# Loading half of each later image as 32-token squares and turning them on VectorE, with the first layer's channels in runs of four per partition

## The chip, the core and the metric

The kernel runs on one core of one Trainium2 chip. The core has five engines that each work through their own instructions in order: TensorE (PE) does the matrix products and the transposes that go through it, VectorE (DVE) and ScalarE (ACT) do elementwise work and read the products out of PSUM, GpSimd (POOL) does elementwise work and issues DMAs, and SyncE (SP) only issues DMAs. Weight loads of PE are listed as an engine of their own (PEld). The metric is the device time of one execution in microseconds.

## The reference, cut to what matters

The input x is eight images of 32 by 32 tokens with 512 channels, in float32. Two layers follow one another. The first normalises x over groups of 16 channels of an image, makes queries, keys and values from it with one 512 x 1536 weight, attends with eight heads of 64 channels, and adds the projected result to x:

```python
def _group_norm(x, scale, bias):
    xg = x.reshape(b, h * w, NUM_GROUPS, c // NUM_GROUPS)
    mu = jnp.mean(xg, axis=(1, 3), keepdims=True)
    var = jnp.var(xg, axis=(1, 3), keepdims=True)
    xn = (xg - mu) * jax.lax.rsqrt(var + EPS)
    return xn.reshape(b, h, w, c) * scale + bias
qkv = _group_norm(x, gn_scale, gn_bias).reshape(b, seq, c) @ w_qkv + b_qkv
weight = softmax(einsum('bhld,bhsd->bhls', q / 8, k / 8))
out = einsum('bhls,bhsd->bhld', weight, v)
x = x + out.transpose(0, 2, 1, 3).reshape(b, seq, c) @ w_out + b_out
```

The second layer (layer norm, a query projection with a depthwise 7 x 7 convolution that gives sampling places, attention to the sampled tokens, and a one-matrix MLP) is not touched. What the change touches is how x reaches the layout that the first layer's products need, with channels on partitions and tokens along the row.

## The kernel before, in words

**Rounds and units.** The first layer goes image by image. A round `b` is the attention of image `b`, and it has `per` = 32 units: four pairs of heads (`hp`) times eight tiles of 128 queries (`qt`). One unit pushes one tile of queries of one head pair: PE makes the scores `sc` (16 matmuls), DVE takes their maxima `nmax` (two reductions over 128 x 1024), ACT takes the exponentials `e` (two of 128 x 1024), DVE turns them in 32 x 32 blocks into `sq` (two more 128 x 1024), SP moves the blocks to their places in `et` by DMA (16 DMAs for two units), and three units later PE multiplies `et` with the values into `av`. There are two PSUM tiles for `sc`, one per head of the pair, so PE can start a unit's scores only when the exponentials of the unit before have been read. There is one PSUM tile for `av`; every fourth unit DVE scales it into `attT`, and only then can the next `av` begin. Beside this, each unit has a place for one more product of PE (`mm`): queries, keys and values of the next head pair, the output projection of the image before, or a chunk of the next layer's convolution input.

**The order is written out by hand.** `at(place, step)` files a step under a place, counted in units from the kernel's first; steps of equal place keep the order in which they were filed. In each unit `push` first gives out the scores, maxima and exponentials, then runs the steps with places up to 0.8 into the unit (`before`), then the two turns of `e` and their DMAs, then the steps from 0.8 to 1 (`after`). So a DVE step at place 10.9 stands behind the turns of unit 10 and ahead of the maxima of unit 11. `nc` is wrapped in `InOrder`, so every engine keeps the order of the program.

**How x gets its layout.** `norm_steps` (line 569) prepares image `b + 1` during round `b`. `turn(t)` takes one tile of 128 tokens x 512 channels, `x`, which `load_x` (line 519) has fetched on POOL's queue in 128 rows of 2 KB; PE transposes its four 128 x 128 parts into a PSUM tile and ACT copies that into `xT` (128 partitions x 4 chunks x 512 tokens, `blk` 0 or 1). There are NX = 2 buffers for `x` and NX_T = 3 for `xT`. Each turn then issues the load of the tile two further on; that DMA stands on POOL's queue and waits until PE has read the buffer. `two_tiles(i)` takes statistics of two turned tiles on DVE (four `bn_stats` of 256 tokens), `gather`, `means`, `deviations` and `factors` make the factors per channel, with two products by `gmat` that sum over groups, and `norm` applies them. The list `norm_places` (line 1001) says when: the eight turns at units 8.4, 8.45, 16.4, 16.45, 22.4, 22.45, 23.4 and 23.45, the statistics at 9.85, 17.86, 22.86 and 23.95, the rest from 23.97 to 26.85. Image 0 is prepared in the same way ahead of round 0.

**What else stands on the engines there.** From round 1's unit 26 on, the next layer's convolution of earlier images runs in the gaps, in chunks (`conv_chunk`, line 919, with `conv_plan`): each of its 49 taps is either a `part_x` of ACT that POOL adds into `oa`, or one `od` instruction of DVE, which reads the padded input `pad_x` and the sum. In rounds 1 to 7 the output projection of the image before runs too (`out_steps`, line 708): per tile a load of `xr` and an addition on POOL, a sum, statistics and `hat` on DVE (`summed` at 0.85 and `norm` at 0.85 of a unit), and two more products of `hat` on POOL.

**Weights.** `w3` holds the three thirds of `w_qkv` with channel `c * 128 + p` on partition `p`, chunk `c`; `gsc` and `gbi`, scale and bias of the group norm, are laid out the same way by `load_cols`.

Of the kernel before, what the change touches and what calls it, by code (L numbers as in the profile page):

```python
# [17 lines left out]
P = 128  # L18
# [230 lines left out]
def attention_then_deformable_attention(  # L249
# [118 lines left out]
    def at(place, step):  # L368
        due.append((place, len(due), step))
# [140 lines left out]
    with ExitStack() as l0:  # L510
# [6 lines left out]
        xs = {}  # L517

        def load_x(b, t):
            if b < B:  # L520
                xs[b, t] = work.tile([P, C], F32, tag="x", name="x", bufs=NX)
                nc.gpsimd.dma_start(xs[b, t], x_tok[b][ts(t, P), :])


        x2 = work.tile([P, NC, QB], F32, tag="xT", name="x2", bufs=NX_T)
# [3 lines left out]
            xs[0, NQT + t] = x2[:, t, :]  # L529
            nc.sync.dma_start(xs[0, NQT + t], x_tok[0][ts(NQT + t, P), :])  # L530
        w3 = [kept(name) for name in ("wA", "wB", "wC")]
        gsc = load_cols(wp, gn_scale, "gsc")
        gbi = load_cols(wp, gn_bias, "gbi")
        bqkv = load_cols(wp, b_qkv, "bqkv")
        for i in (1, 0, 2):
            nc.sync.dma_start(w3[i], by_chunk(w_qkv)[:, :, ts(i, C)])
        bout = load_row(wp, b_out, "bout")
        room_w = {}

# [5 lines left out]
        def load_quarter(w, c):  # L545
# [7 lines left out]

        gmat = wp.tile([P, P], F32, tag="gmat", name="gmat")
        nc.gpsimd.memset(gmat, 1.0 / GRP)
        g3 = gmat.rearrange("p (g c) -> p g c", c=GRP)
        ng = P // GRP
        nc.gpsimd.affine_select(
            out=g3, in_=g3, pattern=[[-GRP, ng], [0, GRP]], compare_op=ALU.is_ge,
            fill=0.0, base=0, channel_multiplier=1,  # L560
        )
        nc.gpsimd.affine_select(
            out=g3, in_=g3, pattern=[[GRP, ng], [0, GRP]], compare_op=ALU.is_ge,
            fill=0.0, base=GRP - 1, channel_multiplier=-1,
        )
        att = MovedAttention(nc, ident, ps_mm, ps_sc, ps_av, work, dram, 1)
        xTs, qkv, vals = {}, {}, {}
# [1 line left out]
        def norm_steps(b, start, places):  # L569

            room = {}

            def turn(t):
                blk, i = divmod(t, NQT)
                if i == 0:
                    xTs[b, blk] = work.tile([P, NC, QB], F32, tag="xT", name="xT", bufs=NX_T)
                if t == 0:
                    room["stats"] = work.tile([P, NC, NT // 2, 6], F32, tag="stats", name="stats", bufs=1)
                ps = mm_tile()
                for c in range(NC):  # L580
                    nc.tensor.transpose(ps[:, ts(c, P)], xs[b, t][:, ts(c, P)], ident)
                nc.scalar.copy(xTs[b, blk][:, :, ts(i, P)], ps.rearrange("p (c q) -> p c q", q=P))
                if b > 0:
                    load_x(b + (t + NX) // NT, (t + NX) % NT)
                elif t < NX:
                    load_x(1, t)

            def two_tiles(i):
                blk, half = divmod(i, NQT // 2)
                for c in range(NC):  # L590
                    nc.vector.bn_stats(
                        room["stats"][:, c, i, :], xTs[b, blk][:, c, ts(half, 2 * P)]
                    )


            def gather():
                mv = room["mv"] = work.tile([P, NC, 2], F32, tag="mv", name="mv")
                stats = room["stats"]
                for c in range(NC):
                    nc.vector.bn_aggr(mv[:, c, :], stats[:, c, :, :].rearrange("p s f -> p (s f)"))  # L600

            def means():
                mv = room["mv"]
                ps = mm_tile()
                for m in range(2):
                    half = ds(m * HD, HD)
                    nc.tensor.matmul(
                        ps[half, 0:NC], lhsT=gmat[:, half], rhs=mv[:, :, 0], start=True, stop=True
                    )
                mu = room["mu"] = work.tile([P, NC], F32, tag="mu", name="mu")  # L610
                nc.vector.tensor_copy(mu, ps[:, 0:NC])
                dev = room["dev"] = work.tile([P, NC], F32, tag="dev", name="dev")
                nc.vector.tensor_tensor(dev, mv[:, :, 0], mu, ALU.subtract)
                nc.vector.tensor_tensor(dev, dev, dev, ALU.mult)
                nc.vector.tensor_tensor(dev, dev, mv[:, :, 1], ALU.add)

            def deviations():
                ps = mm_tile()
                for m in range(2):
                    half = ds(m * HD, HD)  # L620
                    nc.tensor.matmul(
                        ps[half, 0:NC], lhsT=gmat[:, half], rhs=room["dev"], start=True, stop=True
                    )
                room["rs"] = work.tile([P, NC], F32, tag="rs", name="rs")
                rstd(room["rs"], ps[:, 0:NC], 1e-6)

            def factors():
                nc.vector.tensor_tensor(room["rs"], room["rs"], gsc, ALU.mult)
                room["add"] = work.tile([P, NC], F32, tag="nadd", name="nadd")
                nc.vector.tensor_tensor(room["add"], room["mu"], room["rs"], ALU.mult)  # L630
# [15 lines left out]

            steps = [
                *(lambda t=t: turn(t) for t in range(NT)),
                *(lambda i=i: two_tiles(i) for i in range(NT // 2)),
                gather, means, deviations, factors,  # L650
                *(lambda blk=blk: norm(blk) for blk in range(NQB)),
            ]
            for place, what in zip(places, steps):
                at(start + place, what)

        def qkv_steps(b, hp, places):

# [261 lines left out]
        def conv_chunk(b, cb, n):  # L919
# [78 lines left out]
        ]  # L998
        first_values = (1.3, 2.3, 3.3, 4.3)
        value_places = [(-1.7, 2.3, 3.6, 4.3), (10.3, 18.3, 19.3, 20.3)]  # L1000
        norm_places = [
            *(8.4, 8.45, 16.4, 16.45, 22.4, 22.45, 23.4, 23.45),
            *(9.85, 17.86, 22.86, 23.95),
            *(23.97, 24.03, 25.03, 25.81, 25.85, 26.85),
        ]
        out_places = [3.3, 5.3, 6.3, 7.3, 11.3, 13.3, 14.3, 15.3]
# [7 lines left out]
                        start=(c == 0), stop=(c == n - 1),  # L1014
                    )

        norm_steps(0, -100, norm_places)
# [528 lines left out]
```

## Time and profile before

| what | us |
|---|---|
| median of the runs (3 runs) | 3262.32 (3259.76 to 3265.22) |
| the profiled execution | 3264.03 |
| its span, first to last instruction | 3262.3 |
| rounds 2 to 6, from 508.56 to 1821.01 in the span | 1312.45 |
| of these, PE busy | 1311.20 |
| DVE, ACT, POOL busy in them | 1126.55, 835.34, 799.47 |
| 256 transposes of x on PE, whole kernel | 37.5 |
| 64 copies of the turned tiles on ACT | 34.4 (586 ns each) |
| 60 loads of x issued by POOL | 33.3 (557 ns each) |
| 128 statistics of `xT` on DVE | 44.4 (409 ns each) |
| 276 taps `od` on DVE | 232.7 (843 ns each) |

The rows of instruction groups give the time in which at least one of a group was running, and the mean length of one. "Idle before" in such rows is time in which that engine had nothing to do before the instruction, with what ended the wait. In a timeline, the first number is the start in us from the span's beginning, the second the length of the group of like instructions. A busy PE is not PE at its peak, since matmuls are pipelined.

### The profile page before, as it was taken

The page shows a single profiled execution, that of the slowest core. Times are in us where ns is not written, and L with a number is a line of the kernel's source. Part 1 is how long each engine was busy: PE and PEld are TensorE (multiplying, and loading weights), DVE is VectorE, ACT ScalarE, POOL GpSimd, SP SyncE. Part 2 cuts the span into 40 slices and gives each one's busy share as a digit, 9 for nine tenths or more (in the row PEclk, how much of TensorE's full clock was granted, in tenths as well). Part 3 has the DMA queues.
Part 4 walks back from the last instruction along what each step waited for, and adds up shares of the span by engine and source line. Part 5 has one row for each costly group of instructions (what it writes and reads, how often), then busy time and mean ns, then how long its engine had stood idle before and what let it go on. Part 6 is the DMA issues. An engine that isn't in the chain of part 4 may idle for free.

```text
span 3262.3 us, 59564 instructions
## 1 busy us (share of the span) xinstructions
PE 3217.9 (99%) x21588; PEld 1301.2 (40%) x21588; DVE 2522.9 (77%) x3457; ACT 1780.8 (55%) x3826; POOL 1593.5 (49%) x2026
## 2 busy tenths in 40 slices
PE   8999999999999999999999999999999999999999
PEld 4444344344344444444444434333333333333333
DVE  5776778898888888788788888557868787676765
ACT  3443356566567567557657656335555555554442
POOL 1001316755764665664674577225556565653323
PEclk9999999999999999999999999999999999999999
DMA  5666766777677766676676677678777786887873
GB/s 171 169 179 162 210 181 180 211 200 186 204 196 191 203 197 177 204 211 178 181 223 183 177 216 211 180 228 272 219 240 242 228 264 211 264 259 229 265 236 130
DMA packets 479325, 674.31 MB, mean 207 GB/s; under 512 B 76828, under 2 KB 268632, under 8 KB 478776
## 3 DMA queue, kind: packets, MB, share of 16 engines
q1 hardware_dynamic: 434528, 529.53, 56.8%
q0 software_dynamic: 41136, 136.78, 13.7%
q10 hardware_dynamic: 3368, 4.20, 0.4%
q8 instruction: 171, 2.80, 0.4%
q14 instruction: 122, 1.00, 0.1%
HBM read 263.17 MB, written 138.69 MB: 123 GB/s over the span
## 4 chain that ended last, share of the span: by engine, by line
PE 89%; DVE 3%; ACT 2%; DMA 2%; POOL 1%; issue 1%; SPq 1%; POOLq 0%; DVEq 0%; ACTq 0%
PE mm L54 55%; PE sc L54 17%; PE av L54 17%; ACT e L54 1%; DVE nmax L54 1%; SPq L54 1%; DMA et<-sq_d 1%; DVE sq L54 1%; POOL oa L54 0%; DVE chunk L54 0%; DMA w<-in_L_conv_w_out_dram 0%; DMA sq_d<-sq 0%; POOL xr L54 0%; DMA row<-mid,ii 0%; ACT part_x L54 0%
## 5 line engine op out<-in xcount | busy, mean ns | idle before, releaser
L54 ACT ACTIVATE e<-sc,nmax 128x1024 f32<-128x1024 f32 (+1 forms) x1024 | 803.0, 797 | 531.4 <-DVE nmax L54 524.7
L54 DVE TENSOR_REDUCE nmax<-sc 128x1 f32<-128x1024 f32 (+1 forms) x640 | 750.2, 1212 | 291.3 <-PE sc L54 286.0
L54 POOL TENSOR_TENSOR oa<-part_x,oa 128x256 f32<-128x256 f32 x852 | 639.4, 751 | 542.5 <-ACT part_x L54 496.4
L54 DVE STREAM_TRANSPOSE sq<-e 128x1024 f32<-128x1024 f32 x640 | 764.3, 1225 | 118.5 <-ACT e L54 97.7
L54 ACT ACTIVATE part_x<-pad_x,dww_x 128x256 f32<-128x256 f32 x852 | 441.2, 545 | 259.9 <-POOL oa L54 258.4
L54 PE MATMUL sc<-k,q 64*64 64x512 f32 x4096 | 512.3, 603 | 8.8 <-ACT e L54 6.7
L54 PE MATMUL av<-et,v 128*64 128x256 f32 x4096 | 499.2, 386 | 11.7 <-DMA et<-sq 4.5
L54 PEld LDWEIGHTS av<-et,v 128*64 128x64 f32 x4096 | 273.7, 137 | 328.8 <-issue 162.1
L54 POOL TENSOR_TENSOR mv<-mv,minus_half 128x1 f32<-128x1 f32 x128 | 76.3, 596 | 389.0 <-DVE mv L54 388.0
L54 PEld LDWEIGHTS sc<-k,q 64*64 64x64 f32 x4096 | 137.5, 132 | 314.6 <-issue 208.4
L54 POOL TENSOR_TENSOR chunk<-parts,chunk 128x256 f32<-128x256 f32 x240 | 185.3, 772 | 137.2 <-ACT parts L54 123.2
L54 DVE SCALAR_TENSOR_TENSOR od<-pad_x,dww_x,od 128x256 f32<-128x256 f32 x276 | 232.7, 843 | 5.5
L54 PE MATMUL mm<-wo,attH 128*64 128x512 f32 x1024 | 233.7, 598 | 0.0
L54 PE MATMUL mm<-wC,xT 128*64 128x256 f32 x2048 | 232.1, 379 | 0.0
L54 PE MATMUL mm<-xT,wB 128*64 128x512 f32 x1024 | 230.7, 592 | 0.6 <-DVE xT L54 0.6
L54 PE MATMUL mm<-hat_h,wA 128*64 128x512 f32 x1024 | 230.9, 593 | 0.0
L54 PE MATMUL mm<-xT,wA 128*64 128x512 f32 x1024 | 230.7, 592 | 0.0
L54 PE MATMUL mm<-w,attT 128*64 128x512 f32 x1024 | 230.1, 592 | 0.3 <-DMA w<-in_L_conv_w_out_dram 0.3
L54 PE MATMUL mm<-wm,zT 128*64 128x512 f32 x976 | 220.7, 592 | 0.5 <-ACT zT L54 0.5
L54 ACT ACTIVATION_READ_ACCUMULATOR e<-sc,nmax 128x1 f32 x1024 | 209.1, 204 | 0.0
L54 PEld LDWEIGHTS mm<-wC,xT 128*64 128x64 f32 x2048 | 148.0, 137 | 77.7 <-issue 6.4
L54 PE MATMUL mm<-w,hat_x 128*64 128x512 f32 x768 | 170.2, 593 | 0.0
(198 smaller groups left out, 3457.6 us busy)
## 6 DMA issues: line engine op xcount, KB each, us to landing
et<-sq SPq DMA_DIRECT2D x2048, 128.0 KB
sq_d<-sq SPq DMA_DIRECT2D x128, 512.0 KB
et<-sq_d SPq DMA_DIRECT2D x128, 512.0 KB
inv<-rs_d SPq DMA_DIRECT2D x250, 128.0 KB
xr<-mid POOLq DMA_DIRECT2D x64, 256.0 KB
xr<-in_x_dram POOLq DMA_DIRECT2D x62, 256.0 KB
x<-in_x_dram POOLq DMA_DIRECT2D x60, 256.0 KB
out_dram<-res POOLq DMA_DIRECT2D x60, 256.0 KB
```

The lines of the kernel that those rows point to most:

```text
L54: return self.tc.keep_in_program_order(op(*args, **kwargs))
```

## The change

Two kinds of loading take the place of one. For images 1 to 7, the first four tiles (`blk` 0) are fetched by `load_squares` in four DMAs of 64 KB each: DMA `r` brings channels `128 r` to `128 r + 127` of the tile's 128 tokens onto the 32 partitions `32 r` to `32 r + 31`, as four runs of 512 bytes a partition. One DVE transpose in 32 x 32 blocks then writes the tile's part of `xT`, reading every fourth column, with no PE transpose, no PSUM tile and no ACT copy. Partition `p` so holds channels `4 p` to `4 p + 3`, and everything of the first layer that lies along channels follows: the rows of `w_qkv`, `gsc` and `gbi` are loaded in runs of four channels a partition, the PE transposes that remain (image 0, and tiles 4 to 7 of the later images) read every fourth column of `x`, and `gmat` sums over 4 partitions instead of 16, after which a DVE reduction sums the four columns; the factors become one number per partition.

The places move too. In rounds 0 to 6 the four DVE transposes stand at units 1.9, 4.9, 10.9 and 15.9, the first statistics at 11.85 instead of 9.85, the squares of tiles 2 and 3 between 2.6 and 9.6, those of the next image's tiles 0 and 1 between 24.6 and 31.6, and the loads of tiles 4 and 5 at 11.6 and 16.6. The PE turns of tiles 4 to 7 stay at 22.4, 22.45, 23.4 and 23.45.

```diff
         def load_x(b, t):
-            if b < B:
+            xs[b, t] = work.tile([P, C], F32, tag="x", name="x", bufs=NX)
+            nc.gpsimd.dma_start(xs[b, t], x_tok[b][ts(t, P), :])
+
+        def load_squares(b, t, r):
+            if r == 0:
                 xs[b, t] = work.tile([P, C], F32, tag="x", name="x", bufs=NX)
-                nc.gpsimd.dma_start(xs[b, t], x_tok[b][ts(t, P), :])
+            nc.gpsimd.dma_start(
+                xs[b, t][ts(r, SQ)].rearrange("q (s c) -> q s c", s=NSQ),
+                x_tok[b][ts(t, P), ts(r, P)].rearrange("(s q) c -> q s c", s=NSQ),
+            )
...
-        gsc = load_cols(wp, gn_scale, "gsc")
-        gbi = load_cols(wp, gn_bias, "gbi")
+        def load_runs(v, name):
+            t = wp.tile([P, NC], F32, tag=name, name=name)
+            nc.sync.dma_start(t, v.rearrange("(p c) -> p c", c=NC))
+            return t
+
+        gsc, gbi = load_runs(gn_scale, "gsc"), load_runs(gn_bias, "gbi")
...
-            nc.sync.dma_start(w3[i], by_chunk(w_qkv)[:, :, ts(i, C)])
+            nc.sync.dma_start(w3[i], w_qkv.rearrange("(p c) o -> p c o", c=NC)[:, :, ts(i, C)])
...
-        g3 = gmat.rearrange("p (g c) -> p g c", c=GRP)
+        span = GRP // NC
+        g3 = gmat.rearrange("p (g c) -> p g c", c=span)
...
+                if b > 0 and blk == 0:
+                    nc.vector.transpose(
+                        xTs[b, blk][:, :, ts(i, P)].rearrange("p c (s q) -> p s c q", s=NSQ),
+                        xs[b, t].rearrange("p (s i c) -> p s c i", s=NSQ, c=NC),
+                    )
+                    return
                 ps = mm_tile()
                 for c in range(NC):
-                    nc.tensor.transpose(ps[:, ts(c, P)], xs[b, t][:, ts(c, P)], ident)
+                    nc.tensor.transpose(
+                        ps[:, ts(c, P)], xs[b, t].rearrange("p (i c) -> p c i", c=NC)[:, c], ident
+                    )
                 nc.scalar.copy(xTs[b, blk][:, :, ts(i, P)], ps.rearrange("p (c q) -> p c q", q=P))
-                if b > 0:
-                    load_x(b + (t + NX) // NT, (t + NX) % NT)
-                elif t < NX:
-                    load_x(1, t)
+                if b > 0 and t + NX < NT:
+                    load_x(b, t + NX)
...
-                mu = room["mu"] = work.tile([P, NC], F32, tag="mu", name="mu")
-                nc.vector.tensor_copy(mu, ps[:, 0:NC])
+                mu = room["mu"] = work.tile([P, NC], F32, tag="mu", name="mu")[:, 0:1]
+                nc.vector.tensor_reduce(mu, ps[:, 0:NC], AX.X, ALU.add)
...
-                rstd(room["rs"], ps[:, 0:NC], 1e-6)
+                room["one"] = work.tile([P, NC], F32, tag="dev", name="one")[:, 0:1]
+                nc.vector.tensor_reduce(room["one"], ps[:, 0:NC], AX.X, ALU.add)
+                rstd(room["one"], room["one"], 1e-6)
...
+            if b > 0:
+                for t in range(NX):
+                    at(start + load_places[t], lambda t=t: load_x(b, NQT + t))
+                    for r, place in enumerate(square_places[t]):
+                        at(start + place, lambda t=t, r=r: load_squares(b, NX + t, r))
+            if b + 1 < B:
+                for t in range(NX):
+                    for r, place in enumerate(square_places[NX + t]):
+                        place = places[t] + 0.001 if b == 0 else place
+                        at(start + place, lambda t=t, r=r: load_squares(b + 1, t, r))
...
-        norm_places = [
+        first_norm_places = [
             *(8.4, 8.45, 16.4, 16.45, 22.4, 22.45, 23.4, 23.45),
             *(9.85, 17.86, 22.86, 23.95),
             *(23.97, 24.03, 25.03, 25.81, 25.85, 26.85),
         ]
+        square_places = [
+            (2.6, 3.6, 5.6, 6.6),
+            (6.65, 7.6, 8.6, 9.6),
+            (24.6, 25.6, 26.6, 27.6),
+            (28.6, 29.6, 30.6, 31.6),
+        ]
+        load_places = (11.6, 16.6)
+        norm_places = [
+            *(1.9, 4.9, 10.9, 15.9, 22.4, 22.45, 23.4, 23.45),
+            *(11.85, 17.86, 22.86, 23.95),
+            *(23.97, 24.03, 25.03, 25.81, 25.85, 26.85),
+        ]
```

More of the change, by code (lines that the diff above doesn't have):

```diff
@@ L555, in attention_then_deformable_attention @@
         nc.gpsimd.memset(gmat, 1.0 / GRP)
-        g3 = gmat.rearrange("p (g c) -> p g c", c=GRP)
-        ng = P // GRP
+        span = GRP // NC
+        g3 = gmat.rearrange("p (g c) -> p g c", c=span)
+        ng = P // span
         nc.gpsimd.affine_select(
-            out=g3, in_=g3, pattern=[[-GRP, ng], [0, GRP]], compare_op=ALU.is_ge,
+            out=g3, in_=g3, pattern=[[-span, ng], [0, span]], compare_op=ALU.is_ge,
             fill=0.0, base=0, channel_multiplier=1,
@@ L562, in attention_then_deformable_attention @@
         nc.gpsimd.affine_select(
-            out=g3, in_=g3, pattern=[[GRP, ng], [0, GRP]], compare_op=ALU.is_ge,
-            fill=0.0, base=GRP - 1, channel_multiplier=-1,
+            out=g3, in_=g3, pattern=[[span, ng], [0, span]], compare_op=ALU.is_ge,
+            fill=0.0, base=span - 1, channel_multiplier=-1,
         )
@@ L609, in means @@
                     )
-                mu = room["mu"] = work.tile([P, NC], F32, tag="mu", name="mu")
-                nc.vector.tensor_copy(mu, ps[:, 0:NC])
+                mu = room["mu"] = work.tile([P, NC], F32, tag="mu", name="mu")[:, 0:1]
+                nc.vector.tensor_reduce(mu, ps[:, 0:NC], AX.X, ALU.add)
                 dev = room["dev"] = work.tile([P, NC], F32, tag="dev", name="dev")
-                nc.vector.tensor_tensor(dev, mv[:, :, 0], mu, ALU.subtract)
+                nc.vector.tensor_scalar(dev, mv[:, :, 0], mu, None, ALU.subtract)
                 nc.vector.tensor_tensor(dev, dev, dev, ALU.mult)
@@ L624, in deviations @@
                 room["rs"] = work.tile([P, NC], F32, tag="rs", name="rs")
-                rstd(room["rs"], ps[:, 0:NC], 1e-6)
+                room["one"] = work.tile([P, NC], F32, tag="dev", name="one")[:, 0:1]
+                nc.vector.tensor_reduce(room["one"], ps[:, 0:NC], AX.X, ALU.add)
+                rstd(room["one"], room["one"], 1e-6)
             def factors():
-                nc.vector.tensor_tensor(room["rs"], room["rs"], gsc, ALU.mult)
+                nc.vector.tensor_scalar(room["rs"], gsc, room["one"], None, ALU.mult)
                 room["add"] = work.tile([P, NC], F32, tag="nadd", name="nadd")
-                nc.vector.tensor_tensor(room["add"], room["mu"], room["rs"], ALU.mult)
+                nc.vector.tensor_scalar(room["add"], room["rs"], room["mu"], None, ALU.mult)
                 nc.vector.tensor_tensor(room["add"], gbi, room["add"], ALU.subtract)
@@ L1015, in warm @@
                     )
-        norm_steps(0, -100, norm_places)
+        norm_steps(0, -100, first_norm_places)
         for place in (-76.035, -74.5):
```

## The prediction

> **What bounds the kernel now.** I read the page first: how busy each engine is, and which engine the chain that ended last runs through.
>
> ```profile
> PE 3217.9 (99%) x21588; PEld 1301.2 (40%) x21588; DVE 2522.9 (77%) x3457; ACT 1780.8 (55%) x3826; POOL 1593.5 (49%) x2026
> ...
> PE 89%; DVE 3%; ACT 2%; DMA 2%; POOL 1%; issue 1%; SPq 1%; POOLq 0%; DVEq 0%; ACTq 0%
> ```
>
> PE sets the time, and its work shrinks here, so the change looks like a gain. How much is in it shows in PE's timeline of one unit with turns: here unit 16 of round 5 (the round starts at 1296.56).
>
> ```profile
> 1440.47 3.60 PE L54 MATMUL mm<-xT,wA 128*64 128x512 f32 x16
> 1444.01 1.09 PE L54 MATMUL mm<-ident,x 128*128 128x128 f32 x8
> 1445.03 1.52 PE L54 MATMUL sc<-k,q 64*64 64x512 f32 x12
> ```
>
> Two turns hold PE from 1444.01 to 1445.03, 1.02 us. Then I asked who else has no time to spare in the units to which the work goes: busy time by unit, units 11, 12, 13, 15 and 16 of round 5 (the columns: stretch, length, PE, PEld, DVE, ACT, POOL, clock, DMA).
>
> ```profile
> 1393.90:1401.09 7.19, 7.19 (x50) 2.72 (x48) 6.97 (x7) 5.20 (x10) 5.16 (x7) 1.00 0.80 237
> 1401.09:1408.28 7.19, 7.19 (x50) 2.73 (x49) 6.86 (x13) 4.27 (x9) 4.26 (x7) 1.00 0.94 284
> 1408.28:1418.90 10.62, 10.62 (x66) 3.87 (x64) 9.28 (x8) 5.32 (x12) 8.95 (x10) 1.00 0.65 183
> ...
> 1429.56:1436.74 7.18, 7.18 (x50) 2.72 (x48) 4.51 (x6) 4.26 (x9) 5.80 (x7) 1.00 0.70 208
> 1436.74:1445.03 8.29, 8.29 (x59) 3.76 (x57) 7.99 (x14) 4.79 (x10) 6.63 (x8) 1.00 0.66 172
> ```
>
> DVE has 0.2 to 0.3 us left in units 11, 12 and 16. Last, DVE's own order there, and ACT's exponentials after it.
>
> ```profile
> 1396.44 2.34 DVE L54 TENSOR_REDUCE nmax<-sc 128x1 f32<-128x1024 f32 x2
> 1398.92 2.37 DVE L54 STREAM_TRANSPOSE sq<-e 128x1024 f32<-128x1024 f32 x2
> 1401.22 0.65 DVE L54 TENSOR_TENSOR attT<-av,inv 128x512 f32<-128x512 f32 x1
> ...
> 1403.91 2.35 DVE L54 TENSOR_REDUCE nmax<-sc 128x1 f32<-128x1024 f32 x2
> ...
> 1410.10 4.19 DVE L54 SCALAR_TENSOR_TENSOR od<-pad_x,dww_x,od 128x256 f32<-128x256 f32 x3
> 1414.22 2.34 DVE L54 TENSOR_REDUCE nmax<-sc 128x1 f32<-128x1024 f32 x2
> ```
>
> ```profile
> 1406.68 1.10 ACT L54 ACTIVATE e<-sc,nmax 128x1024 f32<-128x1024 f32 x1
> ...
> 1417.70 1.10 ACT L54 ACTIVATE e<-sc,nmax 128x1024 f32<-128x1024 f32 x1
> ```
>
> From 1396.44 to 1414.22 DVE is hardly ever idle. The second exponential of unit 12 ends at 1407.78, and PE starts the next scores, which need its buffer, at 1408.28: 0.50 to spare. In unit 13 it ends at 1418.80 and the scores start at 1418.90: 0.10 to spare. PE looks full, but here DVE is as much the bound.
>
> **What is removed.** In rounds 0 to 6, two turns in unit 8 and two in unit 16: 14 pairs of 1.02 = 14.3 us of PE, if nothing else holds PE. 28 copies of 586 ns leave ACT (16.4 us), which is not the bound. The old POOL waits for PE before loads of x (173.1 us over 13 waits) end; nearly all lie in rounds 0 and 1, where POOL has no taps to do. I count 0 for them.
>
> **What is added on DVE.** Each DVE transpose of x is 128 x 512, reading every fourth float. No row has that read. The nearest two are the turn of `zT` (128 x 512, its writes 16 bytes apart) and the contiguous turn of `sq`:
>
> ```profile
> L54 DVE STREAM_TRANSPOSE zT<-l x57: 1075/1116/1156, 2261.8 to 3196.3; 128x512 f32<-128x512 f32 x57
> ...
> L54 DVE STREAM_TRANSPOSE sq<-e x640: 1195/1229/1249, 38.8 to 3204.9; 128x1024 f32<-128x1024 f32 x160
> ```
>
> Between half of 1.229 = 0.61 and 1.11 us. I take 1.11: same operation, same size, same step of 16 bytes, though on the other side.
>
> The Trainium skill (SBUF — State Buffer, the note on cachelines in "Door 1: The DMA port swizzle") says that reads within a 16-byte line run at full rate and that each step to a new line pays, and yet lists four fp32 as a step that is still free. The `zT` row paid for such a step (1.116 for half the elements of 1.229). By the list the sum below would be some 5 us lower; by the first half of the rule it stands, and PE's reads would pay too.
>
> Now by place. Unit 1.9: DVE waits 0.85 before the maxima of unit 2 (1316.37), and their exponentials leave 1.7 to spare: 0. Unit 4.9: unit 5's maxima start at 1344.28 straight behind three taps, its second exponential ends at 1348.86, the next scores start at 1350.05: 1.19 to spare against 1.11, so 0, but only just. Unit 10.9: unit 11 has 1.16 to spare against 1.11, so again 0. But the delay stays on DVE, and at 11.85 come the statistics of tiles 0 and 1, moved from 9.85 (four in 1.36 us at 1385.03). They are filed before `attT` and `summed` of the same place, so they run ahead of both; behind them wait `attT` (which the next `av` needs; 1.10 to spare), the output sum and unit 12's maxima. These come 1.11 + 1.36 = 2.47 late. What is late next: unit 12's exponentials, unit 13's taps, unit 13's maxima. PE loses 2.47 - 0.50 = 1.97 in front of unit 13 and, with 0.10 spare there, 2.37 by unit 14.
>
> Unit 15.9: again 1.11 ahead of unit 16's maxima, which already start 2.5 us after their first scores are ready. Unit 14's idle PE time cannot be won back, as POOL, ACT and DVE follow each other with 0.08 to spare in unit 15. So unit 16's exponentials come 2.47 + 1.11 = 3.58 late against 0.77 to spare (that spare lies beside the 1.02 of the turn): the next scores start 2.81 late, turn or no turn. Its 1.02 us buy nothing. Unit 18 has 0.42 to spare and can make that 3.16 if the taps of unit 17 pass the delay on whole; its exponentials lose 1.06 of ACT copies (1447.21) in front of them, so I add 0.2.
>
> Per round: -1.02 (unit 8) + 2.81 + 0.2 = +2.0 in rounds 4 to 6. Round 2 has 0.78 to spare in unit 16 and gives the same, +2.0; round 3 has 1.17, +1.6. Five rounds: +9.6. Round 1 has no convolution and only little on DVE: -2.04. In round 0 unit 8's next scores wait for `e` anyway (4.78 us against 4.58 for such a unit without a turn), so nothing comes back there; unit 12's `av` waits for `attT`, now behind the statistics, +1.4; unit 16 gives -1.02. Round 0: +0.4. Together +9.6 - 2.0 + 0.4 = +8.0.
>
> **What is added elsewhere.** POOL issues 112 squares and 32 whole loads of x instead of 60: +84 at 557 ns = 47 us, 12 a round, mostly at .6, between taps that ACT waits for. The units from 24 on have 0.5 to 1.6 to spare in round 5, and in units 9 to 11 POOL waits 1.8 to 5.4 us: 0. If POOL has no such gap, three units a round (28 to 30) could lose up to 0.5 each, 5 x 1.5 = 7.5. The squares wait for a DVE transpose 0.7 units or more before them; taps stand behind them, ACT's `part_x` behind those. They land units ahead of use (4.3 at least, 31 us): 0.
>
> PE's weight loads of the 144 transposes that stay (8 tiles of image 0, 28 of the others) now step 16 bytes. No row has this on PE. The nearest on PE are loads of `smp`, 8 bytes apart: 138 ns against 137. The other bound is the `zT` rate, half. The eight transposes of a pair take 128 ns each; twice that would add 112 x 0.128 = 14.3 us in units 22 and 23, where PE is the bound, and 32 x 0.128 = 4.1 at the start. I take the PE row, 0, and keep 18 for the range. One small reduction more on DVE (0.15) and a power of one column on POOL instead of four (0.60 for 1.04) per image, the shorter `gsc` and `gbi` loads (0.43 and 0.51 on SP at 2.65, ahead of weights that are not waited for), and `w_qkv` in the same 2 KB pieces: 0.3 less at the start, in the rounding.
>
> Sum: 3264.03 + 8 = 3272 for the profiled execution, which lies 1.7 above the median 3262.32; so 3270 for the median.
>
> **Rivals.** (1) The read of every fourth float is free on DVE: 0.61 in place of 1.11 takes 2 x 0.5 a round off five rounds, -5: 3265. For it: taps `od` read every second float and still take 442 ns at least for 256. Against: `zT`. (2) PE pays for the stepped weight loads, point of decision 137 ns becoming more than the 128 between two transposes: with half to all of 18, 3279 to 3288. (3) The other side: DVE's queue takes the additions in its gaps and PE's 14.3 come back, 3248, or half of them, 3255. For it: the places 1.9, 4.9, 10.9 and 15.9 lie in DVE's emptiest units (5.74, 4.99, 5.89 and 4.51 busy), and taps run between 442 and 2358 ns beside POOL, so a shift can shorten them: they need to lose over 2 us a round between units 10 and 17 before it is faster. Against: 0.10 and 0.08 us to spare, round after round, and round 7, which has no turns at all: its unit 16 is 7.19 long with 0.13 to spare, so even there 1.11 us more would lengthen it. That the turns of `blk` 0 leave PE is sure from the code.
>
> Why taps stretch: three took 4.19 us at 1410.10 where POOL added `xr` and `hat`, against 442 ns for the shortest. The Trainium skill (SBUF — State Buffer, "Who interferes with whom") gives the reason: DVE with two SBUF inputs and POOL share a port pair, held for a whole instruction. By it, more POOL work in these units would stretch taps further; squares are not issued in units 12 to 15, so the sum is the same.
>
> **How the numbers follow.** Forecast (DVE's delay eats the gain): 0.40, its own range 3265 to 3278. Rival 1: 0.20. Rival 2: 0.20. Rival 3: 0.20. Faster or slower means by over 0.2%, 6.5 us, about what a measurement of this kernel can tell from no change. Faster: most of rival 3, with a little of 1, 0.19. Same: 0.16 of rival 1, a fifth of the forecast (0.08): 0.24. Slower: the rest, 0.57. The range 3254 to 3285 leaves out the better half of rival 3 and the top of rival 2.
>
> **What would show it.** Right: no PE transposes of x in units 8 and 16; unit 8 at 7.2 us; the x turns on DVE near 1.11 us; unit 12 of rounds 4 to 6 near 9.2 us with PE waiting for `e` or `attT`; unit 16 not shorter than 8.3; units 22 and 23 unchanged at 8.21. Wrong: unit 16 at 7.2 and unit 12 unchanged (rival 3); turns of 0.6 us (rival 1); units 22 and 23 longer (rival 2). A change elsewhere in the span, in the second layer or before 34 us by over 3 us, is in no term of mine.

## The result, and the profile after

| | before | after |
|---|---|---|
| median of 5 runs of each, us | 3265.22 (3259.76 to 3269.47) | 3281.62 (3277.39 to 3286.43) |
| ratio of the two | | 1.0054, 95% interval 1.0038 to 1.0070 |
| a second set, 18 and 6 runs | 3263.42 (3258.66 to 3269.23) | 3277.32 (3272.45 to 3278.78) |
| ratio | | 1.0039, 95% interval 1.0026 to 1.0052 |
| profiled execution, span | 3264.03, 3262.3 | 3283.78, 3282.1 |

The changed kernel is slower by 14 to 16 us. The first two lines below are of the page of the changed kernel (busy time by engine, and the engines of the chain that ended last), the rest of its view of the tile `x` by shape (minimum, median and maximum of one instruction in ns).

```profile
PE 3224.1 (98%) x21476; PEld 1296.8 (40%) x21476; DVE 2552.9 (78%) x3493; ACT 1766.9 (54%) x3798; POOL 1634.7 (50%) x2110
...
PE 82%; POOL 5%; ACT 4%; DVE 4%; DMA 3%; issue 2%; SPq 1%; POOLq 0%; DVEq 0%; ACTq 0%
```

```profile
L54 POOL DMA_DIRECT2D x<-in_x_dram x144: 536/558/707, 1.4 to 1767.7; - x144
L54 PEld LDWEIGHTS mm<-ident,x x144: 195/212/226, 7.5 to 1775.3; 128*128 128x128 f32 x144
...
L54 DVE STREAM_TRANSPOSE xT<-x x28: 1076/1124/1139, 47.4 to 1714.8; 128x512 f32<-128x512 f32 x28
```

PE has 112 matmuls fewer and yet a busy time 6.2 us longer: time in which the matmuls of a group wait for a buffer counts as busy, as unit 13 below shows. The chain runs through PE for 82% instead of 89%; POOL, ACT and DVE have gained what it lost. A DVE turn of x takes 1.12 us, and a weight load of the transposes that are left takes 212 ns where it took 140.

Where the time went is seen unit by unit. A unit is counted from the first matmul of its scores to that of the next unit's. These are units 11 to 17 of round 5 (the round starts at 1304.63), busy time by stretch, columns as before:

```profile
1400.95:1408.14 7.19, 7.19 (x51) 2.73 (x49) 6.98 (x7) 4.41 (x9) 4.58 (x6) 1.00 0.82 233
1408.14:1416.60 8.46, 7.25 (x50) 2.72 (x48) 8.13 (x17) 4.00 (x8) 5.41 (x8) 1.00 0.93 269
1416.60:1427.90 11.30, 11.30 (x66) 4.17 (x64) 9.95 (x9) 5.97 (x12) 8.97 (x10) 1.00 0.66 177
1427.90:1438.96 11.06, 11.06 (x67) 4.05 (x65) 9.94 (x14) 6.48 (x14) 8.16 (x11) 1.00 0.68 179
1438.96:1446.14 7.18, 7.18 (x50) 2.71 (x48) 4.50 (x7) 4.25 (x9) 5.80 (x7) 1.00 0.65 198
1446.14:1453.70 7.56, 7.35 (x50) 2.96 (x48) 7.42 (x13) 3.27 (x8) 5.96 (x7) 1.00 0.61 150
1453.70:1465.45 11.75, 11.69 (x65) 4.05 (x65) 11.37 (x11) 6.95 (x13) 10.05 (x13) 1.00 0.80 264
```

Units 12, 13, 14, 16 and 17 were 7.19, 10.62, 10.65, 8.29 and 10.62 before. DVE's timeline from unit 11 into unit 13 shows why, and PE's beside it where the loss lands:

```profile
1403.48 1.12 DVE L54 STREAM_TRANSPOSE xT<-x 128x512 f32<-128x512 f32 x1
1404.53 2.31 DVE L54 TENSOR_REDUCE nmax<-sc 128x1 f32<-128x1024 f32 x2
1406.98 2.38 DVE L54 STREAM_TRANSPOSE sq<-e 128x1024 f32<-128x1024 f32 x2
1409.28 1.36 DVE L54 BATCH_NORM_STATS2 stats<-xT 128x6 f32<-128x256 f32 x4
1410.56 0.68 DVE L54 TENSOR_TENSOR attT<-av,inv 128x512 f32<-128x512 f32 x1
...
1413.28 2.35 DVE L54 TENSOR_REDUCE nmax<-sc 128x1 f32<-128x1024 f32 x2
```

```profile
1408.14 1.95 PE L54 MATMUL sc<-k,q 64*64 64x512 f32 x16
1411.29 1.95 PE L54 MATMUL av<-et,v 128*64 128x256 f32 x16 [1.21 <-DVE attT L54]
1413.07 3.60 PE L54 MATMUL mm<-xT,wB 128*64 128x512 f32 x16
1416.60 2.63 PE L54 MATMUL sc<-k,q 64*64 64x512 f32 x16
```

The turn at 1403.48 and the statistics at 1409.28 stand in one queue of DVE, with no gap behind them. `attT` begins 2.42 us into unit 12 (0.13 before), the maxima 5.14 us into it (2.82 before). PE waits 1.21 us for `attT`. Then the scores of unit 13 take 2.63 us instead of 1.95: the first half starts when the first exponential of unit 12 has freed its buffer, the second half waits for the other, so the page counts that wait as busy PE.

### The profile page after: what moved, and what is told of

It is laid out like the page before. It is cut to its first block, busy times and chain, and to the rows that moved or that the text cites. A ratio compares the mean times of both kernels' runs of the same rounds, so it can differ in the third digit from the quotient of the medians.

```text
span 3282.1 us, 59491 instructions
## 1 busy us (share of the span) xinstructions
PE 3224.1 (98%) x21476; PEld 1296.8 (40%) x21476; DVE 2552.9 (78%) x3493; ACT 1766.9 (54%) x3798; POOL 1634.7 (50%) x2110
## 4 chain that ended last, share of the span: by engine, by line
PE 82%; POOL 5%; ACT 4%; DVE 4%; DMA 3%; issue 2%; SPq 1%; POOLq 0%; DVEq 0%; ACTq 0%
PE mm L54 52%; PE sc L54 16%; PE av L54 15%; ACT e L54 3%; POOL oa L54 2%; DVE nmax L54 1%; POOL xr L54 1%; DVE sq L54 1%; POOL hat L54 1%; ACT part_x L54 1%; DMA sq_d<-sq 1%; DMA et<-sq 1%; SPq L54 1%; DMA row<-mid,ii 0%; DVE xT L54 0%
## 5 line engine op out<-in xcount | busy, mean ns | idle before, releaser
L54 PE MATMUL sc<-k,q 64*64 64x512 f32 x4096 | 528.8, 603 | 11.9 <-ACT e L54 9.3
L54 POOL DMA_DIRECT2D x<-in_x_dram x144 | 81.2, 566 | 247.1 <-DVE xT L54 139.2
```

The source lines that it names most:

```text
L54: return self.tc.keep_in_program_order(op(*args, **kwargs))
```

## Experiments

The table has the lengths of the units that matter, in round 5 of each profile, and the length of that round; rounding makes some differ by 0.01 from the rows above. Names are those of the runs that follow. The ratio given with a time is that to the kernel before in the same set of runs, with its 95% interval; the medians of the kernel before lie between 3262.7 and 3266.0 in the sets, so times of different sets are compared by their ratios.

| unit | before | after | stats_back | one_unit_earlier | other_places | pairs_share |
|---|---|---|---|---|---|---|
| 8 | 8.21 | 7.19 | 7.19 | 7.19 | 7.66 | 7.19 |
| 9 | 10.62 | 10.62 | 10.62 | 10.62 | 11.01 | 10.62 |
| 12 | 7.19 | 8.47 | 7.19 | 8.46 | 7.19 | 7.19 |
| 13 | 10.62 | 11.30 | 11.26 | 11.30 | 10.62 | 10.62 |
| 14 | 10.65 | 11.05 | 11.24 | 11.05 | 10.89 | 10.68 |
| 16 | 8.29 | 7.56 | 7.54 | 7.27 | 7.25 | 7.28 |
| 17 | 10.62 | 11.74 | 11.75 | 11.01 | 11.01 | 11.01 |
| 22 and 23 | 16.42 | 16.70 | 16.70 | 16.70 | 16.70 | 16.70 |
| 30 | 7.21 | 7.55 | 7.55 | 7.54 | 7.55 | 7.21 |
| round 5 | 262.08 | 264.44 | 263.29 | 263.40 | 262.12 | 260.75 |

### Is DVE's queue the cause?

**stats_back**: the statistics of tiles 0 and 1 go back to 9.85.

```diff
-            *(11.85, 17.86, 22.86, 23.95),
+            *(9.85, 17.86, 22.86, 23.95),
```

> The changed kernel with the statistics of tiles 0 and 1 back at place 9.85. Theory (the additions queue up on DVE between units 10 and 17): of the 2.47 us with which attT and the maxima of unit 12 came late, 1.36 go; unit 12 of rounds 4 to 6 falls from 8.47 to about 7.8, units 12 to 14 lose 1.0 instead of 2.4 against the kernel before, and with round 0's unit 12 the whole time falls by 5 to 8 us, to 3274 to 3277. Rival (POOL's squares and the taps that stand behind them make the stall): unit 12 stays at 8.47, the time within 2 us of the changed kernel's 3281.6.

Measured: 3275.66 us (1.0036, 1.0022 to 1.0050). The ratio lies below the 1.0054 of the changed kernel's first set but hardly below the 1.0039 of its second, so the evidence is in the profile. In round 5 unit 12 is back at 7.19, and units 12 to 14 lose 1.23 instead of 2.36 (29.69 and 30.82 against 28.46). In rounds 3, 4 and 6 the three units together are 1.26 to 1.31 shorter than in the changed kernel. Unit 12 of round 0 falls from 9.60 to 8.31. The rival, POOL, is out as the cause of this half: its squares lie where they lay. The half that is left is about the 1.11 of the turn at 10.9, which this run does not move. In two rounds unit 12 waits for `et`, which comes up again below: 12.61 in round 2 and 8.55 in round 4.

**one_unit_earlier**: one DVE turn from 15.9 to 14.9.

```diff
-            *(1.9, 4.9, 10.9, 15.9, 22.4, 22.45, 23.4, 23.45),
+            *(1.9, 4.9, 10.9, 14.9, 22.4, 22.45, 23.4, 23.45),
```

> The changed kernel with one DVE turn, that of tile 3, at place 14.9 instead of 15.9: in front of the maxima of unit 15, for which DVE waits 0.86 us, instead of those of unit 16, which start late already. Theory (the turn at 15.9 is on the path and the same turn one unit earlier is not): units 16 and 17 of rounds 4 to 6 fall together from 19.30 to 18.2 to 18.5, units 12 to 14 stay at 8.47, 11.30 and 11.27, 4 to 6 us off the time of the changed kernel. Rival (what lengthens unit 17 is POOL or ACT, whose order is the same): 19.3 stays.

Measured: 3271.88 us (1.0021, 1.0008 to 1.0034). Units 16 and 17 together: 18.3 in rounds 4 to 6, where the changed kernel has 19.30; units 12 to 14 as they were. Unit 15 stays at 7.19. So the same 1.1 us of DVE costs PE 1.0 at one place and nothing one unit earlier.

### What do the stepped reads cost?

**contiguous_read**: DVE reads neighbouring floats.

```diff
-                        xs[b, t].rearrange("p (s i c) -> p s c i", s=NSQ, c=NC),
+                        xs[b, t].rearrange("p (s c i) -> p s c i", s=NSQ, c=NC),
```

> The changed kernel, but each DVE turn of x reads 32 neighbouring floats instead of every fourth; the rows of xT of tiles 0 to 3 of images 1 to 7 then belong to other channels than their weights, so the output is not the reference's; sizes and order of all instructions are the same. Theory (the step of 16 bytes on the read side costs DVE half its rate): the turn falls from 1.12 us to about 0.61, and as two of the four turns of a round are on the path, the time falls by 4 to 7 us, to 3275 to 3278. Rival (what costs is the write or a fixed start, the read step is free): the turn stays above 1.0 and the time stays at 3281.

```profile
L54 DVE STREAM_TRANSPOSE xT<-x x28: 669/698/712, 45.9 to 1711.5; 128x512 f32<-128x512 f32 x28
```

The turn takes 698 ns in place of 1124: the step of 16 bytes costs 0.43 us for 512 columns, and the turn without it is not half of the 1.229 for 1024, but 0.70. The time, 3275.21 (1.0040, 1.0027 to 1.0054), cannot show the 4 to 7 us of the theory: the changed kernel's ratios are 1.0054 and 1.0039. The profile is the witness: in round 6, units 12, 13, 14, 16 and 17 sum to 49.46 against 50.32, 0.86 less for two turns (0.84 and 0.89 less in rounds 3 and 4).

**runs_alone**: the kernel before with the weight runs and the stepped PE transposes, and nothing else.

> The kernel before with one part of the change alone: weight rows in runs of four channels a partition, so that all 256 PE transposes of x read every fourth float, and the group means that go with it; no squares, no DVE turns, loads as before. Theory (PE pays for a stepped weight load): units 8, 16, 22 and 23 become 8.35 where they were 8.21 and PE-bound, 28 pairs of 0.14, less where unit 8 and 16 have other waits, and 1.6 at the start: 3 to 6 us more than the kernel before. Rival (the weight load hides behind the transposes): units 22 and 23 at 8.21, no change of more than 1 us.

The transposes of x in the kernel before, then in this run:

```profile
L54 PEld LDWEIGHTS mm<-ident,x x256: 137/140/230, 8.3 to 1762.9; 128*128 128x128 f32 x128
L54 PE MATMUL mm<-ident,x x256: 272/273/475, 8.4 to 1763.0; 128*128 128x128 f32 x128
```

```profile
L54 PEld LDWEIGHTS mm<-ident,x x256: 195/211/230, 7.8 to 1769.1; 128*128 128x128 f32 x128
L54 PE MATMUL mm<-ident,x x256: 273/284/489, 7.8 to 1769.2; 128*128 128x128 f32 x128
```

The weight load rises from 140 to 211 ns, the matmul behind it from 273 to 284; units 22 and 23 go from 8.21 to 8.35, also in the changed kernel. 3267.84 us (1.0019, 1.0009 to 1.0030), in the range of the theory. The start, where the theory put 1.6 us, shows nothing of it: the first scores stand at 34.50 here and at 34.95 and 33.37 in the two profiles of the changed kernel, at 34.35 and 33.54 in those of the kernel before.

### What do POOL's loads cost?

**pool_gap**: the squares of units 24 to 31 move into units 24 to 27.

```diff
-            (24.6, 25.6, 26.6, 27.6),
-            (28.6, 29.6, 30.6, 31.6),
+            (24.6, 25.6, 26.6, 26.61),
+            (26.62, 27.6, 27.61, 27.62),
```

> The changed kernel with the eight squares of units 24 to 31 all in units 24 to 27, where POOL has gaps; all else as it is. Theory (squares between taps cost where POOL, ACT and DVE follow each other closely): unit 30 falls from 7.55 to 7.21 in rounds 2 to 6, nothing else changes: 1.5 to 2.5 us off 3281.6. Rival (unit 30 is longer by DMA traffic or by the start of the next round's buffers): 7.55 stays.

Unit 30 falls from 7.55 to 7.21 in every round from 1 to 5, so squares between taps did cost there. The median, 3277.25, cannot show 2 us: the changed kernel has 3277.32 in the same set.

**other_places**: the same work where DVE has time.

```diff
-            (2.6, 3.6, 5.6, 6.6),
-            (6.65, 7.6, 8.6, 9.6),
+            (1.6, 2.6, 3.6, 4.6),
+            (4.65, 5.6, 6.6, 7.6),
...
-            *(1.9, 4.9, 10.9, 15.9, 22.4, 22.45, 23.4, 23.45),
-            *(11.85, 17.86, 22.86, 23.95),
+            *(0.9, 3.9, 6.9, 9.9, 22.4, 22.45, 23.4, 23.45),
+            *(5.9, 17.86, 22.86, 23.95),
```

> The changed kernel with the same work at other places: DVE turns at 0.9, 3.9, 6.9 and 9.9, statistics of tiles 0 and 1 at 5.9, the squares of tiles 2 and 3 one to two units earlier. In the trace of the kernel before, DVE waits there for the next scores, or the unit has over 3 us to spare. Theory (only the places cost): units 8 and 16 near 7.2 and 7.6, units 12 to 14 as in the kernel before, 7.19, 10.62 and 10.65; each of the rounds 1 to 6 some 1.5 to 1.8 shorter than in the kernel before, less 2 to 3 us for what PE pays at the start and in units 22 and 23: 3250 to 3258 where the kernel before has 3265. Rival (the work itself, POOL's 84 issues and DVE's 28 turns, lengthens the taps wherever it lies): no shorter than 3275.

A miss: 3270.61 (1.0028, 1.0015 to 1.0040), not 3250 to 3258, and not the rival's 3275 or more either. In rounds 5 and 6 units 12 and 13 are as in the kernel before, so DVE's delay is gone there; in rounds 2 and 4 unit 12 takes 10.96 and 9.16, waits for `et`. But units 8 and 9 take 7.66 and 11.01, 0.47 and 0.39 over the 7.19 and 10.62 that they have in the changed kernel. POOL's timeline in unit 5 of round 5 shows a reason:

```profile
1342.16 1.46 POOL L54 TENSOR_TENSOR xr<-xr,bout 128x512 f32<-128x512 f32 x1
1343.56 0.60 POOL L54 DMA_DIRECT2D xr<-in_x_dram  x1
1344.15 1.10 POOL L54 DMA_DIRECT2D x<-in_x_dram  x2
1345.27 1.28 POOL L54 TENSOR_TENSOR hat<-hat,lng_row 128x512 f32<-128x512 f32 x1
1346.62 1.27 POOL L54 TENSOR_TENSOR hat<-hat,lnb_row 128x512 f32<-128x512 f32 x1
1347.85 2.34 POOL L54 TENSOR_TENSOR oa<-part_x,oa 128x256 f32<-128x256 f32 x3
```

Two squares, 1.10 us, stand ahead of the taps `oa`; ACT's `part_x` wait for these, and the exponentials behind `part_x` start 8.27 us into unit 5 instead of 7.24. Unit 5 has 1.19 us to spare for that in the kernel before. In unit 7 they start at 5.32 instead of 3.26, which is more than the 1.68 that unit 7 has. The DVE turn at 6.9 has a part in this: in the next run, which keeps that turn and takes the squares away from there, they start at 3.91.

**pairs**: two tiles share one buffer, so that one DMA brings the squares of both (8 a round instead of 16), in units 1, 26 and 27; two turns at 0.9, the others at 6.9 and 9.9.

```diff
-                xs[b, t][ts(r, SQ)].rearrange("q (s c) -> q s c", s=NSQ),
-                x_tok[b][ts(t, P), ts(r, P)].rearrange("(s q) c -> q s c", s=NSQ),
+                xp["x"][ts(r, SQ)].rearrange("q t (s c) -> q (t s) c", s=NSQ),
+                x_tok[b][ds(t * P, NX * P), ts(r, P)].rearrange("(s q) c -> q s c", s=NX * NSQ),
```

> The changed kernel with two tiles of x in one buffer, so that one DMA brings the squares of two tiles (8 square loads a round in place of 16), issued where POOL is nearly idle (units 1, 26 and 27), DVE turns at 0.9 (two), 6.9 and 9.9, statistics of tiles 0 and 1 at 5.9, whole loads in unit 10. Theory (what the run with other places still lost was POOL: a square of 0.56 us ahead of a tap delays ACT's exponentials of units 5 and 7): units 7 and 8 at 7.19 with at least 0.5 to spare, unit 9 10.62, unit 30 7.21, each of rounds 2 to 6 1.3 to 1.8 shorter than in the kernel before: 3252 to 3258 where that has 3263. Rival (DVE's extra work in units 0 to 10 is enough to lose the gain): units 8 and 9 still 0.8 above 7.19 and 10.62 together, 3268 to 3272.

A miss in the time again, 3273.95 (1.0034, 1.0019 to 1.0049), while units 8, 9 and 30 are 7.19, 10.62 and 7.21 as expected. Unit 3 takes 11.4 to 11.7 (10.64 before), as four loads of 0.58 fell between two taps, and unit 12 takes 12.85, 9.24, 8.46, 7.51 and 8.63 in rounds 2 to 6.

**pairs_early** takes the four loads ahead of the taps of unit 1 and the whole loads of x to unit 18.

```diff
-            (1.602, 1.612, 1.6221, 1.632),
+            (1.012, 1.022, 1.032, 1.042),
...
-        load_places = (10.602, 10.612)
+        load_places = (18.012, 18.022)
```

> The run with pairs, with two things moved: the four square loads of unit 1 ahead of its first taps (place 1.01, where POOL is idle for 5 us) instead of behind them, and the whole loads of x from unit 10 to unit 18, where POOL does nothing. Theory (units 2 and 3 lost 0.8 to 2 us because four loads of 0.58 stood between two taps; unit 12 waited for et, which competed with loads issued in unit 10): units 2 and 3 at 7.21 and 10.64, unit 12 as in the kernel before (7.2 in most rounds), rounds 2 to 6 each 1.3 to 1.8 shorter than in the kernel before, 3254 to 3260 where that has 3263. Rival (the waits of unit 12 come with any more POOL loads): unit 12 still 8 to 13 in most rounds, 3265 or more.

Units 2 and 3 are back at 7.21 and 10.64 in rounds 2 to 6, and the time is 3264.14 (1.0001, 0.9991 to 1.0012). But unit 12 still takes 12.39, 8.29, 13.47, 7.45 and 8.75. In round 4 `av`, which needs the `et` of unit 9, starts 5.44 us into unit 12 instead of 1.9 (unit 9 starts at 1112.44, unit 10 at 1123.06, unit 12 at 1137.46):

```profile
1142.90 3.68 PE L54 MATMUL av<-et,v 128*64 128x256 f32 x16 [3.50 <-DVE rs L54]
1146.34 4.66 PE L54 MATMUL mm<-xT,wB 128*64 128x512 f32 x16
```

The profile puts the wait down to `rs`, which ended just before; `av` does not read it. Where the landing of the last `et` transfer can be followed, in rounds 2 and 4 of stats_back, `av` starts 0.35 us behind it. The wait is also not all that unit 12 loses: behind it `av` and `mm` take 3.68 and 4.66 us instead of 1.95 and 3.60, as PE's granted clock (the share of its full speed, 1.00 in the rows above) is half for 6.83 us (0.75 in the mean of the unit). Over all 14 profiles, from round 1 to the last unit of round 7, none of the 213 waits of PE of 0.15 to 1.98 us was followed by a lower clock; of the 28 waits of 2.0 us or more, 18 were, by 3.41 or 6.83 us at half clock. A long wait for `et` can so cost PE nearly twice its length.

This is the queue of SP, first of the kernel before (unit 9 at 1113.74, unit 10 at 1124.36, unit 12 at 1138.75), then of this run:

```profile
1117.12 0.54 SPq L54 DMA_DIRECT2D mid<-xr  x1
1117.76 0.80 SPq L54 DMA_DIRECT2D hat_d<-hat  x1
1118.65 0.43 SPq L54 DMA_DIRECT2D rs_d<-rsT  x1
1119.18 0.67 SPq L54 DMA_DIRECT2D hat_d<-hat  x1
1121.62 1.28 SPq L54 DMA_DIRECT2D inv<-rs_d  x2
1123.00 13.35 SPq L54 DMA_DIRECT2D et<-sq  x16
```

```profile
1118.41 0.53 SPq L54 DMA_DIRECT2D mid<-xr  x1
1119.04 0.38 SPq L54 DMA_DIRECT2D hat_d<-hat  x1
1119.51 0.41 SPq L54 DMA_DIRECT2D rs_d<-rsT  x1
1120.01 0.53 SPq L54 DMA_DIRECT2D hat_d<-hat  x1
1123.49 1.27 SPq L54 DMA_DIRECT2D inv<-rs_d  x2
1124.87 14.21 SPq L54 DMA_DIRECT2D et<-sq  x16
```

Before, the 16 `et` transfers of units 8 and 9 are issued from 9.26 us into unit 9 on and are out 2.4 us ahead of unit 12. Here they start 12.43 us after unit 9, behind an `inv` that waited for `rs_d` to land, and the last is issued 1.6 us into unit 12. The kernel before falls into the same row of events now and then: in round 4 of its second profile the `et` transfers start 12.57 us into unit 9, and unit 12 takes 12.63. With unit 8 a microsecond shorter, SP has no time left to keep out of it, and it is the usual case.

**pairs_share** tests that: in unit 7 `rs_d` is sent ahead of the `et` transfers instead of behind them.

```diff
+        if early:
+            self.share(u["sums"])
         et = self.moved() if n == 1 else None
```

> The run with pairs loaded early, with one thing more: the sums of unit 7 are turned and sent (rs_d) ahead of that unit's 16 et transfers on SP, not behind them. Theory (what unit 12 waits for is SP: a unit 8 shorter by 1 us leaves it no time, in round 4 rs_d stood behind 16 et transfers of 12.7 us, inv then waited for rs_d to land, and the next 16 et transfers began at 1.81 in unit 10 in place of 9.26 in unit 9): the et transfers of unit 9 start at 8.5 to 9.5 in that unit, unit 12 falls from 7.5 to 13.5 to 7.2 to 8, rounds 2 to 6 are 260 to 261.5 each, the time 3252 to 3259 where the kernel before has 3264. Rival (the et transfers are late because the transfer engines are full in units 11 and 12, 0.8 to 0.94 busy): unit 12 still over 8 in most rounds, 3262 to 3266.

```profile
1117.93 1.59 SPq L54 DMA_DIRECT2D inv<-rs_d  x2
1119.63 13.44 SPq L54 DMA_DIRECT2D et<-sq  x16
```

`inv` no longer waits, and the `et` transfers start 10.31 us into unit 9 (which starts at 1109.32), a little later than the theory put it but early enough: unit 12 takes 8.09 in round 2 and 7.19 in rounds 3 to 6, and the rounds 2 to 6 take 260.75 to 261.23. The rival, full transfer engines, is out: the bytes are the same, and the transfer engines are if anything busier in units 10 and 11 of round 4 (0.90 and 0.87, against 0.83 and 0.83 in pairs_early). The time, 3262.44, is less of a gain than that: 0.9990 (0.9981 to 0.9999) of the kernel before. Round 1 gave back 2.3 against the next run (unit 18 took 12.95, 2.85 of it a wait for `et`, with 3.41 us at half clock behind it), and so did the part from round 7 on, 1.9.

**before_share** is the kernel before with that one move.

> The kernel before with the same early rs_d in unit 7, nothing else changed. Theory (in the kernel before, SP keeps up with a unit 8 of 8.21 except by chance, so there is little to win): within 3 us of the kernel before, fewer long waits in unit 12. Rival (the early rs_d is a gain in itself, whatever turns x): faster than the kernel before by as much as the run with pairs is.

3260.96 us, 0.9991 (0.9982 to 1.0000) of the kernel before. So the early `rs_d` alone is worth as much in the measured time as all of it together, about 3 us by the ratios, as the rival had it, and the two cannot be told apart. Their profiles can: rounds 2 to 6 are 262.1 to 262.7 here and 1.2 to 1.6 shorter with the turns of x on DVE.

### How far do the kernels differ where they are the same?

> The changed kernel once more, for its spread. Theory (the 7 us between the two profiled executions from round 7 on, where both run the same program, are chance waits for transfers, above all et in unit 12 and in the second layer): the stretch from the start of round 7 to the end differs from the 1448.7 us of the first profile by several us, and the waits sit at other units. Rival (something the change left behind makes that stretch longer): 1448 to 1450 again, with unit 17 of round 7 at 12.8 again.

> The kernel before once more, for its spread. Theory (chance waits): from the start of round 7 to the end some us more or less than the 1441.3 of its first profile, rounds 2 to 6 again 262 to 263 each but for single waits for et. Rival (the two kernels differ there): 1441 to 1442 again.

The medians are 3277.32 and 3265.55 (ratios 1.0039 and 1.0002). From the start of round 7 to the end the programs do the same work. The changed kernel took 1448.7 and, again, 1446.0; the kernel before 1441.3 and 1439.0. Over all profiles, those with squares lie between 1440.8 and 1450.2 (ten, mean 1444.7), those without between 1439.0 and 1443.4 (four, mean 1440.9). The two groups overlap, but not in round 7 itself: from its start to that of its last unit they take 262.0 to 266.1 with squares and 260.3 to 261.5 without, and behind it 1178.2 to 1184.6 and 1178.7 to 1182.9. So behind round 7 the theory, chance, can hold; in round 7 it is hardly chance alone. One part was found, in POOL's timeline in unit 16 of round 7 and PE's in unit 17, of the changed kernel:

```profile
1974.17 1.53 POOL L54 TENSOR_TENSOR oa<-part_x,oa 128x256 f32<-128x256 f32 x2 [1.69 <-ACT part_x L54]
1977.35 0.81 POOL L54 DMA_DIRECT2D w<-in_L_conv_wq_dram  x1 [1.65 <-issue]
```

```profile
1986.68 7.09 PE L54 MATMUL mm<-w,hat_x 128*64 128x512 f32 x32 [1.58 <-DMA w<-in_L_conv_wq_dram]
```

POOL stands still for 1.65 us ahead of this load, for nothing that the profile names, and PE then waits 1.58 us for the weights (0.71 in the second profile). The pause is 1.65 in both profiles of the changed kernel and absent in both of the kernel before. Unit 17 takes 12.81 and 11.81 with it, 10.63 and 11.01 without. The rest of the difference, 5 to 6 us, is open.

## Why the prediction was right in sign and short in size

- **The main term held.** DVE's delay of 2.47 us by unit 12 was 2.3; the 2.37 that PE was to lose ahead of unit 14 is 1.96 there and 2.36 by the end of unit 14, in round 5. It lies otherwise than put: 1.28 in unit 12, mostly the wait for `attT`, 0.68 in unit 13 and 0.40 in unit 14, so unit 12 is 8.47 and not 9.2. PE begins the next scores as soon as the first buffer is free and waits in the middle of them, in the next unit; the prediction counted the whole wait ahead of the scores. The two experiments on DVE's places confirm the cause.
- **Unit 16.** It was to be not shorter than 8.3 and is 7.56; unit 17 is 1.12 longer. The sum of both, +0.39, stands against +0.64 forecast; again the wait lies in the scores of the next unit (3.07 us in unit 17, 1.95 before).
- **PE's stepped weight loads**, taken at 0 with 18 as the bound: 0.14 in each of units 22 and 23, 2.0 over seven rounds. The nearest row on PE (`smp`, a step of 8 bytes, 138 ns) misled; the row of the other engine, `zT`, had the right sign. The Trainium skill (SBUF — State Buffer, "Door 1: The DMA port swizzle") lists four fp32 as a step that is still free, beside a rule by which each step to a new line pays; the runs agree with the rule and not with the list, on DVE (1124 ns against 698) and on PE's loads (212 against 140).
- **POOL's issues**, taken at 0 with 7.5 as the bound: 0.34 in unit 30 of rounds 1 to 5, 1.7 together. Each of units 28 to 30 has over 0.5 to spare, as the prediction says, but the delay of one square adds to that of the unit before.
- **The sum by round.** Rounds 2 to 6 were to become 9.6 longer together and became 10.8 longer (in the second pair of profiles 1.7 to 2.2 a round, round 4 left out), of which the two terms above are 2.8. Without them it is 8.0 instead of 9.6, with the waits for `et` that both kernels have in single rounds. Round 1 was to be 2.0 shorter and is 0.9 and 1.2 shorter: units 8 and 16 gave 2.05 back, and units 18, 20, 22, 23 and 30 took part of it. Round 0, forecast +0.4, was +1.85 and -0.3; unit 12's wait for `attT` (+1.29) and unit 16's gain are both there, and unit 4 differs by a wait for `et`.
- **The term that is missing** is that of the end: nothing was counted from round 7 on, where 7 us lie in both pairs of profiles, most of them without a known cause. The 19.8 between the first two profiles are 0.6 ahead of round 0, 1.8 in round 0, -0.9 in round 1, 10.8 in rounds 2 to 6 and 7.4 behind them; the medians are 14 to 16 apart. The forecast's own range ended at 3278: the second median, 3277.32, lies in it, the first above it. The wide range, to 3285, took in a slowdown that the sum did not explain.
- **Rival 3** failed in the changed kernel for the reason that the prediction holds against it, the 0.10 and 0.08 us to spare behind DVE. No part of the prediction had what came next: with DVE's work at other places, POOL's queue (other_places, pairs) and then SP's (pairs_early) kept PE's microsecond, each in turn. Only with all three eased did every one of rounds 2 to 6 get shorter, by 1.2 to 1.6 us against before_share.

## What to carry to other kernels

Moving work from a full engine to one with 20% idle time is worth what the units at the new place can bear: look for the places where the receiving engine waits for the bound engine, and count the whole queue behind each added instruction up to the next unit's start. Where a schedule is tight on several in-order queues, shortening one unit can uncover the next queue, here DVE, then POOL, then SP; follow each queue's first instruction after the shortened stretch and see what it had waited for before. A step of 16 bytes in a read was not free here, on DVE and on PE's weight loads alike.

## What the runs showed of the hardware that was not expected

A weight load of PE with a step of 16 bytes takes 212 ns against 140, and a pair of turns 1.16 us against 1.02, though the matmul that covers it grows by 11 ns only. After 18 of the 28 waits of PE of 2.0 us or more its granted clock was half for 3.41 or 6.83 us, after the 213 of 0.15 to 1.98 us never. POOL's DMA issues pause 1 to 3 us at a few places without a wait that the profile names: the four of the changed kernel lie ahead of the same instructions in both profiles, of the three of the kernel before two came again. They are others with squares than without. The number of issues ahead does not set them: with paired squares, 56 issues fewer, the two behind round 7 stay where they were. SP, which only issues, takes 0.61 us for each `et` transfer at its fastest and 0.89 in the slowest stretch shown (14.21 for 16), and so can be an engine with no time to spare.
